# A searched instruction list, PSUM readers in turn, and filler matmuls behind a branch, in a four-layer graph kernel

## The chip, the cores and the metric

The kernel runs on one core of one Trainium2 chip. The metric is the device time of one execution in microseconds (us); lower is better. The kernel before takes 1670.46 us, the median of three runs (1670.09 to 1670.70).

## The reference

Thirty-two graphs of 512 nodes with 128 features each pass through four residual layers. All layers use the same 512x512 matrix `adj` of zeros and ones.

```python
# layer 0: edge scores
h   = relu(layernorm(x));  xh = elu(h @ Wi + bi)
e   = sigmoid(xh @ We_tgt[:, None] + xh @ We_src[None, :] + be) * mask(adj)
own = xh * e.sum(-1)
recv = elu(concat(e @ xh, own) @ Wn + bn)
x  += concat(recv, xh) @ Wm + bm
# layer 1: five steps of a gated update, h = relu(layernorm(x)) at the start
m = adj @ h;  z, r = sigmoid(gates of m, h);  c = tanh(m-part + (r*h) @ u5.T)
h = (1 - z) * h + z * c          # five times, then x += h
# layer 2: x += adj @ (relu(layernorm(x)) @ W) + b
# layer 3: x += sum over k of adj^k @ h @ W_k, k = 0..3
```

## The kernel before

**Staging.** The kernel never loops on the chip. Python code lists some thousand operations, each on a whole 128x512 tile or a piece of it, and a planner written in the kernel (class `Plan`) turns the list into one order, which is then emitted as it stands. Each operation (`Op`, made by `Plan.op`, L61) has an engine, a guessed duration, a due time, the values it reads and writes, and with these the operations that must be listed before it. `Plan.order` (L121) is a list scheduler: it walks through planned time, and whenever an engine is free it gives that engine the ready operation with the earliest due time, provided that buffers are free. The due times come from a pace: one graph begins every 14 us at first (`FIRST_PACE`) and every 56 us later (`PACE`). Many graphs are therefore under way at the same time, each in another layer.

The order of each engine's queue is fixed when the program is built. On the chip, semaphores alone decide when an instruction starts; an instruction that waits holds up everything behind it on its own engine. The planner's guessed times never appear on the chip.

**Buffers.** PSUM has eight banks, the kind `b`. One of them, `spare`, is taken out of the pool at L304 and serves as the target of filler matmuls: `plan.idle` (L306, printed as line L307) multiplies `ones` by `ones`. In the part of the list before the branch the planner puts a filler wherever TensorE has nothing to do. The bank goes back into the pool at planned time `BRANCH` = 18 us (L738).

**The branch.** The kernel counts whether `adj` survives rounding to a shorter format (L520, L541, L546; the count is `inexact`). The operations planned for the first 18 us stand ahead of a branch on that count (L1003, L1004). Behind it stand two arms, one for an exact and one for an inexact matrix. With the data at hand the exact arm runs. All later work is in the arm.

**Layer 0 of the first graphs** is what the early part consists of. For each graph: a product with `Wi` (L449), the first `elu`, a product with the token weights (L593), a spread of the scores (L630), four tanh (L645) and four masked products on VectorE (L648), four matmuls that gather messages (L656), a product with `ones` or `ones_r` for the sums (L449, L690), the value `own` (L693), a product with `Wn` (L449), the second `elu`, whose last step (L566) is the value `recv`, and eight matmuls with `Wm` (L703) whose sum is added to x (L469). The transposed weights of layer 1 are made on the way (L761, L763), and a permuted copy of the matrix, AQ (L845, L848).

**elu** (L549 to L568) reads one PSUM bank three times: exp and tanh on ScalarE, and the linear part, max(v + bias, 0). The linear part is VectorE's (L559) for the first two graphs' first elu and ScalarE's (L562) everywhere else.

**Steady work.** Layer 1's step has five products with a 128x128 weight (L449: u3T, w4T, w3T, w5T, u5T), eight fp32r matmuls with the matrix (L857), copies out of PSUM by ScalarE (L438), sums by VectorE (L882 and others). Layer 3 is L938 and L947.

Of the kernel before, what the change touches and what calls it, by code (L numbers as in the profile page):

```python
# [2 lines left out]

# [38 lines left out]
class Plan:  # L42
# [7 lines left out]
    def __init__(self, slots, ahead, last):  # L50
        self.ahead, self.last, self.ops, self.vals = ahead, last, [], {}
        self.free = {k: [(0.0, i) for i in range(n)] for k, n in slots.items()}
        self.until = dict.fromkeys(self.RESULT, 0.0)
        self.shared, self.now = 0.0, 0.0
        self.careful = 0.0
        self.slack = 0.0
        self.pieces = {}
        self.cold = 4.5
        self.idle = None

    def op(self, eng, us, due, emit, reads=(), writes=(), two=None, keep=0, result=None,  # L61
           earliest=0.0, margin=0.0):

        two = eng == "POOL" if two is None else two
        o = Op(eng, us, self.RESULT[eng] if result is None else result, emit, two, keep)
        o.earliest, o.margin = earliest, margin
        for v in reads:  # L70
            o.before.add(v.writer)
        for v in writes:
            o.before.update(v.readers)
            if v.writer:
                o.before.add(v.writer)
            elif v.kind and v.slot is None:
                o.takes.append(v)
        for v in reads:
            v.readers.append(o)
        for v in writes:  # L80
            v.writer, v.readers = o, []
        o.vals = [v.whole or v for v in dict.fromkeys([*reads, *writes])]
        for v in o.vals:
            v.left += 1
        for v in [*reads, *writes, *o.vals]:
            self.vals[v] = True
        o.before -= {o, None}
        o.due = max([due, *(b.due for b in o.before)])
        for b in o.before:
            b.after.append(o)  # L90
        self.ops.append(o)
# [28 lines left out]
    def order(self, end=None):  # L120

        left = [o for o in self.ops if not o.begun]
# [5 lines left out]
        coming, ready = {e: [] for e in self.until}, {e: [] for e in self.until}  # L128
        order, events, index = [], [self.now], {}
# [25 lines left out]
        while events:  # L155
            now = heapq.heappop(events)
            if end is not None and now >= end:
                break
            for e in self.until:
                while coming[e] and coming[e][0][0] <= now:  # L160
                    _, i, o = heapq.heappop(coming[e])
                    heapq.heappush(ready[e], (o.due, i, o))
                if self.until[e] > now:
                    continue
                passed, o = [], None
                while ready[e] and o is None:
                    x = heapq.heappop(ready[e])
                    if begins(x[2], now):
                        o = x[2]
                    else:  # L170
                        passed.append(x)
                for x in passed:
                    heapq.heappush(ready[e], x)
                if o is not None and now < self.careful and any(
                    c.due < o.due and t < now + 0.3 * o.us for t, _, c in coming[e]
                ):
                    heapq.heappush(ready[e], (o.due, index[o], o))
                    o = None
                if o is None and e == "PE" and end is not None and self.idle.known <= now:
                    order.append(self.idle)  # L180
                    self.until[e] = now + self.idle.us * (1.9 if now < self.cold else 1.0)
                    heapq.heappush(events, self.until[e])
                if o is None:
                    continue
                order.append(o)
                o.begun = True
                while oldest + 1 < len(by_due) and by_due[oldest].begun:
                    oldest += 1
                o.start, self.until[e] = now, now + o.us
                if o.two:  # L190
                    self.shared = self.until[e]
                for v in o.takes:
                    v.slot = self.free[v.kind].pop(self.clean(now) if v.added else 0)[1]
                    if v.kind == "b":
                        self.pieces[v.slot] = v.pieces
                o.known = self.until[e] + o.result
                heapq.heappush(events, self.until[e])
                heapq.heappush(events, o.known)
                for v in o.vals:
                    v.left -= 1  # L200
                    if not v.left and v.kind:
                        self.free[v.kind].append((o.known, v.slot))
                        self.free[v.kind].sort()
                for a in o.after:
                    if a in index:
                        a.waits -= 1
                        a.ready = max(a.ready, self.known(o, a))
                        if not a.waits:
                            heapq.heappush(coming[a.eng], (a.ready, index[a], a))
                            heapq.heappush(events, a.ready)  # L210
        assert end is not None or len(order) == len(left), "the plan does not end: too few buffers"
        self.now = end or 0.0
        return order


@with_exitstack
def tile_four_graph_layers(
# [33 lines left out]
    assert D == P and G * D == 512 and N == 512 and K == 7  # L251

    PACE, FIRST_PACE, LAST_PACE = 56.0, 14.0, 30.0
    BRANCH = 18.0
    MARGIN = 10.0
    FIRST = 2

# [4 lines left out]
    plan = Plan(slots, ahead=60.0, last=(B - 2) * PACE)  # L262
# [33 lines left out]
    def chunks(t):  # L296
# [9 lines left out]
    plan.free["b"].pop()  # L306
    plan.idle = Op("PE", 0.224, 0.0, lambda: nc.tensor.matmul(  # L307
        spare[:, :P], at(ones), at(ones), start=True, stop=True), False, 0)
    plan.idle.known = 0.4
    op("POOL", 0.2, -9, lambda: nc.gpsimd.memset(at(neg_half), -0.5), [], [neg_half])  # L310
    ones_r = const("ones_r", [P, P], F32R)
    op("POOL", 0.4, 5, lambda: nc.gpsimd.tensor_copy(at(ones_r), at(ones)), [ones], [ones_r])
# [45 lines left out]
    Wm_sb = load_const(Wm.rearrange("(t p) o -> p t o", p=P), [P, 2, P], "Wm_sb", -5)  # L358
    bm_bc = load_const(bm.partition_broadcast(P), [P, P], "bm_bc", -5, earliest=BRANCH)
    load_graph(3, -6, 3.6)  # L360
# [362 lines left out]
    def issue(operations):  # L723
        with tc.manual_schedule():
            for o in operations:
                o.emit()
# [6 lines left out]
    def arm(exact):  # L733
        with ExitStack() as stack:
            pool = stack.enter_context(tc.tile_pool(name=f"arm{exact:d}", bufs=1))
            plan.back_to(common)
            plan.slack = 0.3
            plan.free["b"].append((BRANCH, len(places["b"]) - 1))  # L738
            list_rest(exact, pool)
            issue(plan.order())  # L740

    def list_rest(exact, pool):
        n = 25 if exact else 16
# [260 lines left out]
    with tc.If(taken < 1) as branch:  # L1004
        arm(True)
# [42 lines left out]
```

## Time and profile before

| | |
|---|---|
| three runs | 1670.09, 1670.46, 1670.70 us |
| profiled execution, its own time | 1668.0 us |
| its span, first to last instruction | 1666.2 us |
| outside the span | 1.8 us |
| TensorE clock granted | 1.0 throughout |
| end of the last matmul to the end of the span | some 5.3 us |

The profile is of one execution. PE is TensorE, DVE is VectorE, ACT is ScalarE, POOL is GpSimd and SP issues most of the DMAs. A row of a timeline gives start, length, engine, line, operation, tiles and a count; brackets give the engine's idle time just before it and what ended that. One fp32 product of 128x512 appears as two matmul records. A matmul's recorded length runs past the start of the next one, so the time that a matmul takes from the engine is read from one start to the next.

### The profile page before, as it was taken

The page shows a single profiled execution, that of the slowest core. Times are in us where ns is not written, and L with a number is a line of the kernel's source. Part 1 is how long each engine was busy: PE and PEld are TensorE (multiplying, and loading weights), DVE is VectorE, ACT ScalarE, POOL GpSimd, SP SyncE. Part 2 cuts the span into 40 slices and gives each one's busy share as a digit, 9 for nine tenths or more (in the row PEclk, how much of TensorE's full clock was granted, in tenths as well). Part 3 has the DMA queues.
Part 4 walks back from the last instruction along what each step waited for, and adds up shares of the span by engine and source line. Part 5 has one row for each costly group of instructions (what it writes and reads, how often), then busy time and mean ns, then how long its engine had stood idle before and what let it go on. Part 6 is the DMA issues. An engine that isn't in the chain of part 4 may idle for free.

```text
span 1666.2 us, 21483 instructions
## 1 busy us (share of the span) xinstructions
PE 1655.3 (99%) x6585; PEld 1071.5 (64%) x6585; DVE 1429.3 (86%) x3344; ACT 1131.0 (68%) x2133; POOL 237.7 (14%) x240
## 2 busy tenths in 40 slices
PE   9999999999999999999999999999999999999998
PEld 6555556656666666666666666666666666666787
DVE  8889999999988898889888898888999888877842
ACT  7877677877766677667666677676768666655640
POOL 2211101212111110111111111101121110000100
PEclk9999999999999999999999999999999999999999
DMA  3444434543445434454434454444454543222202
GB/s 99 122 112 142 133 113 109 134 123 112 133 115 139 123 112 114 105 137 127 127 102 112 123 134 115 120 117 118 129 137 128 127 126 96 89 64 89 83 14 60
DMA packets 284925, 188.05 MB, mean 113 GB/s; under 512 B 77312, under 2 KB 237952, under 8 KB 284800
## 3 DMA queue, kind: packets, MB, share of 16 engines
q1 hardware_dynamic: 270688, 162.98, 32.7%
q0 software_dynamic: 12528, 22.81, 8.2%
q8 instruction: 54, 0.88, 0.2%
q10 hardware_dynamic: 1584, 0.79, 0.2%
q14 instruction: 71, 0.58, 0.1%
HBM read 82.78 MB, written 73.33 MB: 94 GB/s over the span
## 4 chain that ended last, share of the span: by engine, by line
PE 97%; ACT 2%; DVE 1%; issue 0%; ACTq 0%; DVEq 0%
PE b L449 44%; PE b L857 21%; PE b L947 11%; PE b L938 7%; PE b L656 6%; PE b L703 3%; PE b L920 2%; PE b L593 2%; PE b L690 1%; PE b L307 1%; ACT f L495 0%; ACT f L454 0%; ACT f L645 0%; PE b L378 0%; DVE f L648 0%
## 5 line engine op out<-in xcount | busy, mean ns | idle before, releaser
L438 ACT COPY f<-b 128x512 f32<-128x512 f32 x356 | 206.5, 586 | 147.9 <-PE b L857 103.8
L857 PE MATMUL b<-AQ,r 128*128 128x512 f32 x1024 | 304.7, 439 | 0.0
L486 POOL TENSOR_TENSOR s<-s,nhalf 128x4 f32<-128x4 f32 x128 | 155.9, 1218 | 897.1 <-DVE s L484 795.9
L857 PEld LDWEIGHTS b<-AQ,r 128*128 128x128 f32 x1024 | 192.1, 188 | 90.2 <-issue 51.4
L882 DVE TENSOR_TENSOR f<-f,b 128x512 f32<-128x512 f32 x320 | 211.6, 676 | 26.7 <-PE b L449 24.8
L390 DVE STREAM_TRANSPOSE f<-f 128x512 f32<-128x512 f32 x246 | 206.7, 844 | 20.9 <-ACT f L495 20.3
L947 PE MATMUL b<-r,A_r 128*128 128x512 f32 x768 | 223.9, 426 | 0.0
L454 ACT ACTIVATE f<-f,b4w 128x512 f32<-128x512 f32 x160 | 115.3, 723 | 156.1 <-DVE f L882 155.4
L495 ACT ACTIVATE f<-x,s 128x128 f32<-128x128 f32 x504 | 207.3, 489 | 16.3 <-DVE s L490 16.0
L947 PEld LDWEIGHTS b<-r,A_r 128*128 128x128 f32 x768 | 139.3, 189 | 46.6 <-issue 24.4
L449 PE MATMUL b<-f,u3T 128*128 128x512 f32 x320 | 163.1, 593 | 1.1 <-DVE f L882 0.9
L449 PE MATMUL b<-f,w4T 128*128 128x512 f32 x320 | 163.1, 593 | 0.2 <-ACT f L438 0.2
L449 PE MATMUL b<-f,u5T 128*128 128x512 f32 x320 | 162.7, 592 | 0.2 <-DVE f L889 0.2
L449 PE MATMUL b<-f,w5T 128*128 128x512 f32 x320 | 162.4, 592 | 0.0
L449 PE MATMUL b<-f,w3T 128*128 128x512 f32 x320 | 162.2, 592 | 0.0
L857 PE MATMUL b<-A_r,r 128*128 128x512 f32 x512 | 149.0, 433 | 0.0
L899 DVE TENSOR_TENSOR f<-f,f 128x512 f32<-128x512 f32 x160 | 109.0, 681 | 43.2 <-ACT f L454 42.9
L938 PEld LDWEIGHTS b<-V,f 128*128 128x128 f32 x1024 | 131.0, 191 | 21.2 <-issue 15.6
L680 POOL DMA_DIRECT2D f<-f x87 | 78.0, 897 | 458.7 <-DVE r L831 71.7
L454 ACT ACTIVATE f<-b,b5w 128x512 f32<-128x512 f32 x160 | 109.5, 685 | 48.0 <-PE b L449 47.1
L831 DVE TENSOR_TENSOR r<-f,r 128x512 fp32r<-128x512 f32 x192 | 130.2, 680 | 8.3 <-ACT r L827 8.2
L454 ACT ACTIVATE f<-f,b3w 128x512 f32<-128x512 f32 x160 | 114.9, 720 | 27.2 <-DVE f L882 26.4
(112 smaller groups left out, 2539.8 us busy)
## 6 DMA issues: line engine op xcount, KB each, us to landing
m<-f SPq DMA_DIRECT2D x246, 256.0 KB, 2.1
f<-m SPq DMA_DIRECT2D x186, 256.0 KB, 2.9
f<-f POOLq DMA_DIRECT2D x87, 256.0 KB, 3.6
f<-m SPq DMA_DIRECT2D x240, 64.0 KB, 2.5
x<-in_x_dram SPq DMA_DIRECT2D x32, 256.0 KB, 3.3
f<-f SPq DMA_DIRECT2D x29, 256.0 KB, 2.4
f<-d SPq DMA_DIRECT2D x28, 256.0 KB, 5.3
out_dram<-x SPq DMA_DIRECT2D x28, 256.0 KB, 2.4
```

What stands on the lines that cost most here:

```text
L390: op("DVE", us, due, lambda: nc.vector.transpose(view_out(at(blocks)), view_in(at(src))), [src], [blocks])
L438: op("ACT", us, due, lambda: nc.scalar.copy(at(t), at(src)), [src], [t])
L449: nc.tensor.matmul(to, at(w), of, start=start, stop=stop)
L454: op("ACT", us, due, lambda: nc.scalar.activation(at(dst), at(src), AF.Tanh, bias=at(bias), scale=scale), [src, bias], [dst])
L486: op("POOL", 1.35, due, lambda: nc.gpsimd.tensor_tensor(stat(SCALE), stat(VAR), at(neg_half), op=ALU.pow), [s, neg_half], [s])
L495: nc.scalar.activation(at(h)[:, ts(c, P)], at(X[b])[:, c, :], AF.Relu, bias=stat(SHIFT)[:, c : c + 1], scale=stat(SCALE)[:, c : c + 1],)
L831: op("DVE", T_VEC, due, lambda: nc.vector.tensor_tensor(part(lo), whole(), part(hi).bitcast(F32), op=ALU.subtract), [src, hi], [lo], two=two)
L857: nc.tensor.matmul(at(pa), at(part)[:, ts(jc, P)], view(at(columns)[:, jc, :]), start=jc == n == 0, stop=jc == NC - 1 and n == PARTS - 1,)
L882: op("DVE", T_VEC, d, lambda: nc.vector.tensor_tensor(at(s), at(u), at(pg), op=ALU.add), [u, pg], [s])
L899: op("DVE", T_VEC, d, lambda c=c, h=h: nc.vector.tensor_tensor(at(c), at(c), at(h), op=ALU.subtract), [c, h], [c], two=True)
L938: nc.tensor.matmul(at(pz)[:, ts(i, D)], at(hT[i])[:, ts(ic, P)], at(V[k]), start=i == 0, stop=last and i == G - 1,)
L947: nc.tensor.matmul(at(pz), at(adjT)[:, jc, ts(ic, P)], at(part), start=False, stop=jc == NC - 1 and n == PARTS - 1,)
```

## The change

1. **Readers of a bank in turn.** `Plan.op` now also makes an operation that reads a PSUM bank come after the bank's previous reader, if that one is on another engine. For the first two graphs' first elu this puts the VectorE linear part behind exp and tanh.
2. **Filling behind the branch.** Fillers are planned up to time `FILL` = 50 us instead of up to the branch, and are left out if a TensorE operation becomes ready within one filler's length. The spare bank goes back into the pool at 50 us instead of 18 us.
3. **A searched list.** In the exact arm, the due times of all operations due before 130 us are varied at random 240 times (a shift for one engine or all in a stretch of time, or a shift for 1 to 10% of the operations). The planner lists the arm for each variant, and the variant whose planned end is earliest is kept. The search runs while the program is built and costs no device time.

The lines of `elu` itself are the same in both kernels: the linear part on VectorE for the first two graphs was there before.

```diff
     def op(self, eng, us, due, emit, reads=(), writes=(), two=None, keep=0, result=None,
...
         for v in reads:
             o.before.add(v.writer)
+            if v.kind == "b" and v.readers and v.readers[-1].eng != eng:
+                o.before.add(v.readers[-1])
...
-                if o is None and e == "PE" and end is not None and self.idle.known <= now:
+                if o is None and e == "PE" and self.idle.known <= now < self.fill and not (
+                    coming[e] and coming[e][0][0] < now + self.idle.us):
                     order.append(self.idle)
...
+    def searched_order(self, until, rounds):
+        ops = [o for o in self.ops if not o.begun]
+        early, rng, asked = [o for o in ops if o.due < until], random.Random(3), self.state()
+
+        def listed(due):
+            self.back_to(asked)
+            for o, d in zip(early, due):
+                o.due = d
+            return self.order()
+
+        best, first = None, [o.due for o in early]
+        due = first
+        for _ in range(rounds):
+            try:
+                listed(due)
+                end = max(o.start + o.us for o in ops)
+                if best is None or end <= best[0]:
+                    best = end, due
+            except AssertionError:
+                pass
+            due = [*best[1]]
+            if rng.random() < 0.5:
+                start, width = rng.uniform(15, until), rng.uniform(2, 15)
+                shift, eng = rng.gauss(0, 4), rng.choice(["PE", "ACT", "DVE", None, None])
+                varied = {i: shift for i, o in enumerate(early)
+                          if start <= first[i] < start + width and eng in (None, o.eng)}
+            else:
+                n = max(1, int(len(early) * rng.uniform(0.01, 0.1)))
+                varied = {i: rng.gauss(0, 4) for i in rng.sample(range(len(early)), n)}
+            for i, shift in varied.items():
+                due[i] += shift
+        return listed(best[1])
...
-    BRANCH = 18.0
+    BRANCH, FILL = 18.0, 50.0
...
-    plan.idle.known = 0.4
+    plan.idle.known, plan.fill = 0.4, FILL
...
-            plan.free["b"].append((BRANCH, len(places["b"]) - 1))
+            plan.free["b"].append((FILL, len(places["b"]) - 1))
             list_rest(exact, pool)
-            issue(plan.order())
+            issue(plan.searched_order(130.0, 240) if exact else plan.order())
```

The two built programs can be laid side by side, engine by engine. In the arm that runs, TensorE has the same 4469 matmul instructions in both, counted without fillers. Fillers: 46 before, all ahead of the branch; 69 after, 42 ahead of it and 27 behind. Their runs after the change are 21, 3, 3, 5, 2 and 8 ahead of the branch and 3, 1, 8, 9, 1 and 5 behind. The last 745 matmul instructions stand in the same order, kind by kind, in both.

More of the change, by code (lines that the diff above doesn't have):

```diff
@@ L2 @@
 import heapq
+import random
 import concourse.bass as bass
@@ L58, in __init__ @@
         self.cold = 4.5
+        self.fill = 0.0
         self.idle = None
@@ L210, in order @@
                             heapq.heappush(events, a.ready)
-        assert end is not None or len(order) == len(left), "the plan does not end: too few buffers"
+        assert end is not None or all(o.begun for o in left), "the plan does not end: too few buffers"
         self.now = end or 0.0
         return order
+    def searched_order(self, until, rounds):
[28 more added lines that the diff above has]
+        return listed(best[1])
 @with_exitstack
```

## The prediction

> **What bounds the kernel now.** First the page's engine shares and the chain of work that ended last:
>
> ```profile
> PE 1655.3 (99%) x6585; PEld 1071.5 (64%) x6585; DVE 1429.3 (86%) x3344; ACT 1131.0 (68%) x2133; POOL 237.7 (14%) x240
> ...
> PE 97%; ACT 2%; DVE 1%; issue 0%; ACTq 0%; DVEq 0%
> ```
>
> TensorE bounds the kernel. So the time is the matmuls' own time, which the change leaves alone, plus fillers, plus TensorE's stalls, plus the ends. Next TensorE's waits, all that the profile shows (total, times, longest):
>
> ```profile
> PE b L703 <- DVE f L566: 1.8, 2, 1.2
> PE b L307 <- DVE ones L302: 1.0, 1, 1.0
> PE b L449 <- DVE f L882: 0.9, 1, 0.9
> PE b L761 <- ACT f L562: 0.8, 1, 0.8
> PE b L656 <- DVE f L648: 0.3, 1, 0.3
> PE b L449 <- DVE f L889: 0.2, 1, 0.2
> PE b L449 <- ACT f L869: 0.2, 1, 0.2
> PE b L449 <- ACT f L438: 0.2, 1, 0.2
> ```
>
> Only 5.4 us in 1666. Asked by stretch, the waits for L566, L562, L648 and L869 (3.1 us) lie between 20 and 70 us, those for L882, L889 and L438 (1.3 us) between 350 and 400. Nothing else waits until the last matmul. A matmul's record outlasts its slot, so these numbers are too small; starts tell more. The timeline around the worst wait:
>
> ```profile
> 27.24 1.06 PE L593 MATMUL b<-W_tok,f 128*128 128x130 f32 x8
> 28.13 0.49 PE L761 MATMUL b<-ident,f 128*128 128x128 f32 x3
> 29.38 0.33 PE L761 MATMUL b<-ident,f 128*128 128x128 f32 x1 [0.76 <-ACT f L562]
> 29.64 0.65 PE L630 MATMUL b<-ident,s 128*128 128x128 f32 x4
> 31.51 2.05 PE L703 MATMUL b<-Wm_sb,f 128*128 128x128 f32 x16 [1.22 <-DVE f L566]
> 33.40 0.60 PE L378 MATMUL b<-ident,f 128*128 128x128 f32 x4
> ```
>
> Four L630 records take 0.44 us from start to start, so L703 could have begun at 30.1: the stall is 1.4 us, not 1.22. Taking the regular spacing of each kind (0.43 us per half product, 0.11 per 128-wide record, 0.23 per fp32r matmul) from all starts, the stalls are: 0.4 at L449 Wn (26.3), 1.1 around L761 (29.4), 1.5 at L703 (31.5), 0.3 and 0.1 at 36.5 to 41, 0.8 at the second L703 (46.0), 0.6 at L656 (62.1), 0.4 at u3T (63.5), with small remainders **5.4 us** between 20 and 70 us. From 350 to 400 us they are **2.1 us**, the largest here:
>
> ```profile
> 383.26 1.02 PE L449 MATMUL b<-f,Wi_sb 128*128 128x512 f32 x2
> 385.22 1.13 PE L449 MATMUL b<-f,u3T 128*128 128x512 f32 x2 [0.94 <-DVE f L882]
> ```
>
> That 7.5 us is all that a better order can remove; elsewhere TensorE is full. Fillers, of which all 46 lie before 18.9 us:
>
> ```profile
> 12.02 1.28 PE L307 MATMUL b<-ones 128*128 128x128 f32 x10
> 13.23 0.34 PE L541 MATMUL b<-ones,n_odd 128*1 128x1 f32 x8
> ```
>
> Five fillers take 1.21 us here; from filler to filler it is 0.22.
>
> **What the Trainium skill says.** "TensorE: Matmul & The Clock Gate", Part 1: the array starts at half clock, reaches full clock after about 3.4 us of work, and falls back only after an idle window of about 3.4 us. The trace agrees: filler records start 0.21 us apart until 5.7 us and 0.11 after. Behind the branch the longest idle is 1.22 us and the spacing after it stays at 0.11. So filling behind the branch has no clock to save.
> "PSUM — Partial Sum Buffer", PSUM bank collisions: two engines must not touch one bank at once, and software has to keep them apart, reads against reads too. The kernel's program did so already, without the planner's knowledge: ScalarE's exp waits for VectorE's linear part.
>
> ```profile
> 10.91 0.75 DVE L559 TENSOR_SCALAR f<-b,bi_sb 128x512 f32<-128x512 f32 x1 [1.60 <-PE b L449]
> ...
> 11.69 0.69 ACT L554 ACTIVATE f<-b,bi_sb 128x512 f32<-128x512 f32 x1 [0.57 <-DVE f L559]
> ```
>
> "Trainium Kernel Development and Optimization", Reading a trace, calls matmul busy time a bad metric because matmuls are pipelined. The trace agrees (L449's u3T records last 0.59 us on average at 0.43 spacing); hence starts above.
>
> **The change, part by part.**
> *Fillers.* 23 more, each an instruction that TensorE executes whether or not it would have waited: 23 x 0.222 = **+5.1 us**. Work that a stall would have covered hides them; without a stall they are pure cost.
> *Readers in turn* adds no wait on the chip that was not there. In graph 0's elu the linear part moves behind tanh. Before, L559, exp, tanh, L564 and L566 ran from 10.91 to 14.41. After, exp starts when ScalarE is through its last cast and mask scaling at about 10.8, tanh ends at 12.0, and VectorE, which has graph 1's normalization ahead (1.03 us of L501), does linear part, L564 and L566 from 12.5 to 14.3. The same end: 0.
> *The branch.* `inexact` now stands behind three mask steps and two score steps on VectorE: written at 14.4 before, about 16.6 after. SP issued its first load behind the branch 1.06 us after that (15.53), so all of SP's queue there (weights, biases, graphs 4 and 5) comes about 2.1 us later. The first users are VectorE's L759 and L481 and TensorE's L761 at 23.9 to 25.7; w4's load would land at about 19.2 + 2.9 = 22.1. Covered by 1.8 us. POOL, ACT, DVE and PE have work queued across the branch as before: 0.
> *The order.* I followed the new queues by the durations of this profile (VectorE 0.60 per full tile, ScalarE 0.57, statistics 1.26, a product 0.86, four transposes 0.44). Reaching the first L703, TensorE has done the same real work in both orders: before 31.51 - 8.30 - 24 fillers (5.3) - stalls 2.8 = 15.1 us. After, with one filler fewer at the start, it is 8.1 + 15.1 + 42 fillers (9.3) + 0.15 (a transpose waiting for graph 1's normalization) = **32.6**. Is `recv` there? Wn ends at 27.6, exp, tanh and linear part end at 29.5, L564 at 29.6, then the list has graph 3's statistics (1.26) ahead of L566: 31.5. The fillers outlast it by 1.1 us. Second L703: before 46.02, of it 13.0 real work since the first; after 32.6 + 13.0 + 6 fillers (1.3) = **46.9**; `recv` by ScalarE's queue (L495 for graph 1's layer 1 stands ahead of exp) at 46.0. Outlasted again, by 0.9. So stalls up to there vanish (4.3 us) and fillers take their place and more. Then up to 70 us I find the producers ahead of every use by 0 to 1 us, 0.2 us of stalls where 1.0 was. Sum at 70 us: +5.1 - 5.4 + 0.4 = **+0.1**. My walk can err by a microsecond per chain, and errors only add stalls: +0.4 taken, bounds -0.3 (no stall left) and +5.1 (all stalls stay).
> *Later.* Between 350 and 400 us the new list puts Wi earlier and other work between Wn and the next u3T, so the wait at 385 loses its place. But VectorE is 94% busy from 200 to 400 (140.5 us of 150, 47.2 of 50), and a list off by a little finds another wait. The trace does not show the new ones; bounds 0 and 4 us, taken 1.1 in place of 2.1: **-1.0**.
> *The ends.* The last 745 matmul instructions, 212 us by the spacings above, stand in the same order; the start's wait for `ones` stays: 0.
> Sum: +0.4 - 1.0 = **-0.6 us**. Against the profiled execution: span 1665.6, with the 1.8 us outside 1667.4. The profiled execution lies 2.5 us under the median of the runs, so I take the difference to the median: 1670.46 - 0.6 = **1669.9**.
>
> **The rivals.**
> *A. Fillers for stalls, later waits halved:* 1669.9, own range 1668.9 to 1671.1.
> *B. The later wait goes and none comes:* stalls at 70 us even, -2.1, with the walk's +0.1: 1668.4. For it: one place held nearly all of it, and the list changed there. Against: VectorE's load.
> *C. The later waits grow instead:* two or three waits of 1.2 us among VectorE's backlog between 60 and 480 us, +0.4 + 1.5: 1672.4.
> *D. Slower: fillers come on top of the stalls.* Place: the two L703. If `recv` is later than I found, by other waits on ScalarE's and VectorE's queues, TensorE runs its 27 fillers and still waits. With all stalls kept: 1670.5 + 5.1 = 1675.6. It decides from `recv` being late by the margins (1.1 and 0.9) plus about 3 us in sum. For it: a search fits the list to guessed times and leaves no slack. Against: the guesses (0.61, 0.6, 0.86) are near the measured durations.
> That the change does nothing to elu's linear part is plain from the diff; that item is no part of any sum.
>
> **How the numbers follow.** Measurement tells about 0.2% (3.3 us) from no change. A 0.50, B 0.22, C 0.18, D 0.10. Faster by over 0.2% needs 1667.1, below B's bound of -0.3 - 2.1 = 1668.1: 0.03 for what I overlook. Slower needs 1673.8: D and the far end of C less D's near end, 0.11. Range 1667.9 to 1673.4: it takes in A, B and most of C and leaves D out.
>
> **What would show it.** Right: L307 records 138 (twice 69), about 18 us in all; TensorE's waits for L566 and L562 gone or under 0.3 us; the first L703 at about 32.6, the second at 46.9; waits behind 70 us at most 2 us. Wrong: L703 still waiting behind its fillers (D), new waits of TensorE for VectorE between 60 and 480 us (C), or matmul spacings that changed.

## The result and the profile after

The changed kernel takes 1667.67 us, the median of 20 runs (1666.05 to 1668.86). The kernel before, run beside it, takes 1670.05 us (20 runs, 1667.43 to 1672.00). The ratio is 0.9987, 95% interval 0.9981 to 0.9993: faster by 2.4 us between the medians, and by 2.2 us (1.2 to 3.2) by the ratio, which is estimated from all the runs. The prediction said 1669.9 and a range from 1667.9, so the change gained about 2 us more than its sum, and the median lies 0.2 us under the range.

The profiled execution of after has an own time of 1666.99 us and a span of 1665.2. First the page's engine shares and the head of its chain of work:

```profile
PE 1657.5 (100%) x6631; PEld 1076.8 (65%) x6631; DVE 1428.9 (86%) x3344; ACT 1127.5 (68%) x2133; POOL 236.8 (14%) x240
...
PE 96%; DVE 2%; DMA 1%; ACT 1%; issue 0%; DVEq 0%
```

TensorE counts as busy for the whole span, rounded; the 46 more matmul records are the 23 fillers, each listed twice. The waits of TensorE in after, all that the profile shows (total, times, longest):

```profile
PE b L348 <- DVE ones L343: 1.0, 1, 1.0
PE b L697 <- DVE f L689: 0.5, 1, 0.5
PE b L634 <- DVE f L923: 0.2, 1, 0.2
```

Of the eight rows of before, the one for `ones` stays, the one for the masked product (L656 before, L697 now) stays, and the other six are gone. The one new row is 0.2 us at 384.6 us. The lines named here stand 41 lower down in the file than before. The timeline at the place where before had its worst wait (L802 is the transpose that was L761, L744 the product with `Wm` that was L703, L348 a filler):

```profile
28.12 0.27 PE L802 MATMUL b<-ident,f 128*128 128x128 f32 x1
28.23 1.95 PE L348 MATMUL b<-ones 128*128 128x128 f32 x16
30.02 0.27 PE L802 MATMUL b<-ident,f 128*128 128x128 f32 x1
30.13 2.17 PE L348 MATMUL b<-ones 128*128 128x128 f32 x18
32.14 0.27 PE L802 MATMUL b<-ident,f 128*128 128x128 f32 x1
```

Seventeen fillers (34 records) stand where TensorE waited before. `recv` for the first L744 is done at 31.50 (L607, 30.82 + 0.68), as predicted; L744 starts at 32.25, where 32.6 was predicted, without a wait. The second L744 starts at 46.60 (predicted 46.9).

The place of the worst later wait of before, at 385 us, looks like this in after (L490 was L449, L731 was L690, L634 was L593):

```profile
377.09 1.02 PE L490 MATMUL b<-f,Wi_sb 128*128 128x512 f32 x2
378.04 0.73 PE L731 MATMUL b<-q,ones_r 128*128 128x512 f32 x2
...
382.93 1.02 PE L490 MATMUL b<-f,u3T 128*128 128x512 f32 x2
383.79 0.61 PE L634 MATMUL b<-W_tok,f 128*128 128x130 f32 x4
384.64 0.71 PE L634 MATMUL b<-W_tok,f 128*128 128x130 f32 x4 [0.24 <-DVE f L923]
385.19 1.02 PE L490 MATMUL b<-f,w3T 128*128 128x512 f32 x2
```

The product with `Wi` now stands 6 us ahead of the one with `u3T`, which no longer waits. Instead the eight records of L634 take 1.40 us from start to start in place of 0.89: by starts, the new wait is 0.5 us and not 0.2.

So the early part went as predicted and brought nothing. To see where the gain is, I take the same accounting as the prediction's: TensorE's starts, less the regular spacing of each kind of matmul. What is left is waiting, cold start and a drift of my spacings of about 0.37 us per 100 us, the same in all kernels. The table gives it for three profiled executions of before and two of after (the repeats are experiments below); "tail" runs from the last matmul's start to the end of the span.

| us | fillers | waits to 70 us | 70 to 600 | behind 600 | last matmul starts | tail | span |
|---|---|---|---|---|---|---|---|
| before | 10.26 | 8.32 | 4.56 | 3.72 | 1660.47 | 5.73 | 1666.20 |
| before, second | 10.26 | 8.28 | 4.78 | 4.42 | 1661.35 | 6.52 | 1667.88 |
| before, third | 10.26 | 8.74 | 4.81 | 4.97 | 1662.39 | 6.49 | 1668.88 |
| after | 15.39 | 3.41 | 2.77 | 3.65 | 1658.84 | 6.35 | 1665.19 |
| after, second | 15.39 | 3.56 | 2.16 | 3.65 | 1658.37 | 5.94 | 1664.31 |

Fillers and early waits together: 18.6, 18.5, 19.0 before and 18.8, 18.95 after, a change of about +0.2 us by the means. These columns hold the cold start too: 22, 22 and 26 of the first filler records are about 0.21 us apart in place of 0.11 in before, 17 and 21 in after. By the means that is some 0.4 us in favour of after which the change did not make. Between 70 and 600 us: -2.25 by the means. Behind 600 us: -0.7. The gain is late. It lies in waits behind 70 us, while the last filler is planned for 50 us.

### The profile page after: what moved, and what is told of

Read it like the earlier page. It is cut to its first block, busy times and chain, and to the rows that moved or that the text cites. A ratio compares the mean times of both kernels' runs of the same rounds, so it can differ in the third digit from the quotient of the medians.

```text
span 1665.2 us, 21541 instructions
## 1 busy us (share of the span) xinstructions
PE 1657.5 (100%) x6631; PEld 1076.8 (65%) x6631; DVE 1428.9 (86%) x3344; ACT 1127.5 (68%) x2133; POOL 236.8 (14%) x240
## 4 chain that ended last, share of the span: by engine, by line
PE 96%; DVE 2%; DMA 1%; ACT 1%; issue 0%; DVEq 0%
PE b L490 43%; PE b L898 21%; PE b L988 11%; PE b L979 7%; PE b L697 6%; PE b L744 3%; PE b L961 2%; PE b L634 2%; PE b L348 1%; PE b L731 1%; DMA m<-f 0%; DVE f L431 0%; DVE f L923 0%; DVE r L872 0%; DMA f<-m 0%
## 5 line engine op out<-in xcount | busy, mean ns | idle before, releaser
L898 PEld LDWEIGHTS b<-AQ,r 128*128 128x128 f32 x1024 | 192.1, 188 | 89.4 <-issue 51.4
L490 PE MATMUL b<-f,w4T 128*128 128x512 f32 x320 | 163.2, 592 | 0.0
L490 PE MATMUL b<-f,u3T 128*128 128x512 f32 x320 | 163.1, 592 | 0.0
L490 PE MATMUL b<-f,u5T 128*128 128x512 f32 x320 | 162.9, 592 | 0.0
L490 PE MATMUL b<-f,w5T 128*128 128x512 f32 x320 | 162.8, 592 | 0.0
L490 PE MATMUL b<-f,w3T 128*128 128x512 f32 x320 | 162.3, 592 | 0.0
```

Source lines behind the costliest of these rows:

```text
L490: nc.tensor.matmul(to, at(w), of, start=start, stop=stop)
L898: nc.tensor.matmul(at(pa), at(part)[:, ts(jc, P)], view(at(columns)[:, jc, :]), start=jc == n == 0, stop=jc == NC - 1 and n == PARTS - 1,)
```

## The experiments

Medians beside the kernel before on the same chip; ratios with 95% intervals. The gain or loss in microseconds is the difference of the two medians; the ratio is estimated from all the runs, and differs from the quotient of the medians by up to 0.0005. Waits by stretch come from one profiled execution of each kernel.

**What comes and goes in the kernel before.** No edit.

> The kernel before, unchanged, profiled a second time. Theory T (TensorE is full, so the time is fixed matmul work plus fillers plus stalls, and the first profile, 2.5 us under the median, caught an execution with few stalls): median 1670.0, and the second profile shows another sum of stalls than the first, with the later stalls (60 to 600 us, 3.2 us in the first) differing by 1 us or more while the early ones (20 to 60 us) repeat within 0.3. Rival: stalls repeat within 0.3 us everywhere, and executions differ in what lies outside the matmuls.

1668.85 us against 1669.20, ratio 1.0003 (0.9995 to 1.0011). The waits up to 70 us repeat within 0.15 us and those at 358, 360 and 385 us within 0.05 us, so these belong to the list; the expected difference of 1 us or more before 600 us did not show. But the profile has two more, at 726 and 728 us, which its first profile lacks (the timeline of this execution):

```profile
726.09 1.12 PE L449 MATMUL b<-f,u5T 128*128 128x512 f32 x2
727.05 1.05 PE L938 MATMUL b<-V,f 128*128 128x128 f32 x8
728.31 1.12 PE L449 MATMUL b<-f,w4T 128*128 128x512 f32 x2 [0.20 <-ACT f L438]
```

By starts they and the ones beside them cost 0.77 us, and the tail is 0.8 us longer. So what differs between these two executions lies behind 600 us.

**Are the fillers behind the branch pure cost?** The fillers are taken out of, or doubled in, the finished list of the changed kernel, so that nothing else moves.

```diff
-            issue(plan.searched_order(130.0, 240) if exact else plan.order())
+            listed = plan.searched_order(130.0, 240) if exact else plan.order()
+            issue([o for o in listed if o is not plan.idle])
```

> The changed kernel with its 27 fillers behind the branch not emitted; order otherwise the same. Theory T: the fillers stand where TensorE would wait, and outlast the waits by 0.7 us (recv of graph 0 at 31.5, its matmuls at 32.25) and 0.6 us (46.0 and 46.6): without them waits of 4.7 us come back and the kernel gains 1.3 us, 1666.4. Rival F (filling itself brings the gain, by clock or otherwise): 1670 or slower. Rival P (fillers are pure cost): 6.0 us faster, 1661.7.

1667.85 us against 1669.20, ratio 0.9996 (0.9988 to 1.0005). It is not faster than the full change (0.9987) but, if anything, about 1 us slower, although 6.0 us of fillers are gone. The theory that they are pure cost falls. Theory T missed as well, by 1.4 us: it had no term for the clock. The timeline of this kernel shows the waits that came instead (L803 is the transpose, L744 the product with `Wm`):

```profile
29.21 0.33 PE L803 MATMUL b<-ident,f 128*128 128x128 f32 x1 [1.19 <-ACT f L603]
31.52 0.33 PE L803 MATMUL b<-ident,f 128*128 128x128 f32 x1 [1.98 <-ACT f L686]
31.68 3.25 PE L744 MATMUL b<-Wm_sb,f 128*128 128x128 f32 x16
34.73 0.98 PE L419 MATMUL b<-ident,f 128*128 128x128 f32 x4
```

Two waits of 3.2 us in sum, as expected of a list without fillers. But the sixteen L744 records take 3.05 us from 31.68 to 34.73, where before's sixteen take 1.89 (31.51 to 33.40). The stretches say why (columns: stretch, its length, TensorE's busy time and instructions, granted clock, DMA share, GB/s):

```profile
31.00:32.00 1.00, 0.48 (x4) 1.00 0.00 0
32.00:33.00 1.00, 1.00 (x7) 0.54 0.00 0
33.00:34.00 1.00, 1.00 (x7) 0.50 0.00 0
34.00:35.00 1.00, 1.00 (x7) 0.50 0.00 0
35.00:36.00 1.00, 1.00 (x6) 0.75 0.00 0
```

TensorE ran at half clock from 32 to 35.5 us: 0.46 + 0.50 + 0.50 + 0.25 = 1.7 us lost, behind waits of which none was over 2 us by the records. Up to 70 us the waits of this kernel are 10.51 us against 3.41 with the fillers: 7.1 us more, of it 1.7 from the clock, for 6.0 us of fillers saved.

```diff
-            issue(plan.searched_order(130.0, 240) if exact else plan.order())
+            listed = plan.searched_order(130.0, 240) if exact else plan.order()
+            issue([x for o in listed for x in ([o, o] if o is plan.idle else [o])])
```

> The changed kernel with each of the 27 fillers behind the branch emitted twice. Theory T: no wait is left for them to stand in, so they cost their length, 27 x 0.222 = 6.0 us: 1673.7. Rival (fillers are hidden by something): under 1670.

1672.28 us against 1669.20, ratio 1.0020 (1.0012 to 1.0029). 27 x 0.222 = 6.0 us of fillers are added, the waits up to 70 us stay (3.51 against 3.41), and the last matmul starts 5.5 us later than in after, the rest being 0.6 us less between 70 and 600. Where nothing waits any more, a filler is paid in full.

**One part of the change at a time.** From the kernel after, each part is undone by one of these edits; for the readers in turn alone, that part was added to the kernel before.

No readers in turn:

```diff
-            if v.kind == "b" and v.readers and v.readers[-1].eng != eng:
-                o.before.add(v.readers[-1])
```

No filling behind the branch:

```diff
-                if o is None and e == "PE" and self.idle.known <= now < self.fill and not (
-                    coming[e] and coming[e][0][0] < now + self.idle.us):
+                if o is None and e == "PE" and end is not None and self.idle.known <= now:
...
-    BRANCH, FILL = 18.0, 50.0
+    BRANCH, FILL = 18.0, 18.0
```

No search:

```diff
-            issue(plan.searched_order(130.0, 240) if exact else plan.order())
+            issue(plan.order())
```

Search alone (readers in turn and filling undone):

> The kernel before with the searched list alone: no readers in turn, fillers (46) only ahead of the branch, spare bank back at 18 us. Theory T: the search shortens some of the 5.4 us of early stalls and moves the later ones; 1668.5, between the two kernels. Rival S (the searched list is the whole gain, the other two parts cost): 1667.0 or below. Rival N (without readers in turn the search fits a plan that does not hold): 1670 or slower, with early stalls of 5 us or more.

Filling and readers in turn, no search:

> The changed kernel without the search: readers in turn and fillers behind the branch (35 in the arm, 42 ahead of it, 77 in all), list as the planner first makes it. Theory T2 (the gain is waits behind 70 us that the searched list does not have; up to 70 us fillers and stalls trade evenly): no gain, 1669.0 to 1671.0 on the scale where the kernel before takes 1669.2 to 1670, with waits of 1.5 us or more between 70 and 600 us. Rival (turns and fillers bring the gain): 1667.7 or below.

Readers in turn alone:

> The kernel before with readers in turn alone, no search, fillers (43) only ahead of the branch. Theory T2: within 1 us of the kernel before, unless the list behind 70 us happens to change, in which case by the change of the waits there. Rival C (readers in turn makes a worse list): 1.5 us slower or more.

Readers in turn and search, no filling:

> Readers in turn and search, fillers (43) only ahead of the branch, bank back at 18 us. Theory T2: as the search alone, 3 to 4 us faster than the kernel before (ratio 0.998), waits behind 70 us under 0.7 us. Rival C (readers in turn costs what the full change lacks against the search alone): ratio 0.9987 like the full change. If it is as fast as the search alone, it is the fillers and the withheld bank that cost the full change its 1.4 us.

Filling alone:

> Fillers behind the branch and the bank withheld until 50 us, alone: no readers in turn, no search (42 fillers ahead of the branch, 23 behind). Theory T3 (fillers cost their length, 19 more than in the kernel before = 4.2 us, and take the place of waits; they gain only where the waits would drop the TensorE clock, which the list of the kernel before does not do): fillers and waits up to 70 us sum to 18.6 to 19.6 us as against 18.6, time within 1.5 us of the kernel before. Rival F (filling gains by itself): 2 us faster.

Filling and search, no readers in turn:

> The full change without readers in turn. Theory T3: the gain is the search's, and without readers in turn the list is as good as with the search alone: 3 to 4 us faster than the kernel before, full clock throughout. Rival C2 (readers in turn is what makes the search's plan hold once fillers are there): no faster than the full change, ratio 0.9987 or above.

| parts | median, before beside it | ratio (interval) | fillers + waits to 70 us | 70 to 600 | behind 600 |
|---|---|---|---|---|---|
| search alone | 1665.42, 1669.20 | 0.9978 (0.9972 to 0.9985) | 17.97 | 2.14 | 3.93 |
| filling + search | 1666.36, 1668.82 | 0.9982 (0.9975 to 0.9990) | 19.70 | 2.08 | 3.65 |
| all three (the change) | 1667.67, 1670.05 | 0.9987 (0.9981 to 0.9993) | 18.80 | 2.77 | 3.65 |
| filling alone | 1670.06, 1668.82 | 1.0004 (0.9995 to 1.0012) | 18.90 | 5.45 | 3.65 |
| filling + turns | 1670.77, 1669.13 | 1.0007 (0.9999 to 1.0016) | 20.85 | 2.83 | 5.44 |
| turns alone | 1671.15, 1669.13 | 1.0013 (1.0005 to 1.0021) | 23.58 | 4.17 | 3.66 |
| turns + search | 1671.84, 1669.13 | 1.0016 (1.0008 to 1.0023) | 20.94 | 7.00 | 4.01 |

The "fillers + waits" column holds the cold start: from 14 (filling alone) to 29 (turns + search) of the first filler records at half-clock spacing, by an estimate from these counts up to 1.5 us between two rows, so smaller differences in that column tell nothing.

The gain is the search's: every kernel that is faster than before has it, and taking it from the change takes the gain away (filling + turns, 1.0007). The search alone is the fastest of all by its median, 3.8 us under before; its interval and the change's just overlap. A search is no warrant of a gain, though: with the readers in turn and no filling it is slower than before, against both expectations. Of the others, rival S held for the search alone and rival C for turns alone, and filling + search gained 2.5 us where 3 to 4 were expected.

Filling alone gives nothing that can be told from none. Readers in turn alone cost 2.0 us. They bunch the waits: in its profile, an execution 1.75 us over its median, between 30 and 50 us that kernel waits 1.10, 1.68, 1.58 and 0.67 us, and the clock falls to half twice (34.3 to 37.8 and 48 to 51.4 us). The stretches of that execution:

```profile
34.00:35.00 1.00, 1.00 (x8) 0.67 0.00 0
35.00:36.00 1.00, 1.00 (x7) 0.50 0.00 0
36.00:37.00 1.00, 1.00 (x4) 0.50 0.00 0
37.00:38.00 1.00, 1.00 (x3) 0.62 0.00 0
48.00:49.00 1.00, 1.00 (x5) 0.50 0.59 174
49.00:50.00 1.00, 1.00 (x7) 0.50 0.06 16
50.00:51.00 1.00, 1.00 (x6) 0.50 0.00 0
51.00:52.00 1.00, 1.00 (x8) 0.80 0.00 0
```

With the search but without fillers, the readers-in-turn kernel has one wait of 2.86 us at 33.6, one stretch at half clock after it (34.6 to 38.0 us), and some 4.4 us of new waits between 70 and 130 us; this profile lies 1.6 us over its median. With fillers the readers' order has no cost that can be told (all three against filling and search: the intervals overlap). So the parts do not add. What the filling does for the readers' order is shown in part: added to turns + search it takes 2.1 us off up to 70 us (some 1.2 of it the cold start), where it keeps the clock, but 4.2 us off between 70 and 600 us, where there are no fillers and the search found another list. Whether that is the filling's doing or the luck of another list was not tried.

The table shows one thing more. Against filling + turns, the list without the search, the change gains 2.05 us up to 70 us (some 0.5 of it the cold start) and 1.8 us behind 600, and little between (2.83 against 2.77). That the search gains in the later waits holds against the kernel before.

**Does any search do it, or this one?** The seed of the random variation is 4 in place of 3.

```diff
-        early, rng, asked = [o for o in ops if o.due < until], random.Random(3), self.state()
+        early, rng, asked = [o for o in ops if o.due < until], random.Random(4), self.state()
```

Search alone with seed 4:

> The search alone with another random sequence (4 in place of 3). Theory T2 with a search that works: 2.5 to 4 us faster than the kernel before, waits behind 70 us under 0.7 us again. Rival L (luck: any other list has other waits): anywhere from 1 us slower to 4 us faster, waits behind 70 us of 1 us or more.

1667.25 us against 1669.13, ratio 0.9988 (0.9982 to 0.9995). Half the gain of seed 3: this list keeps a wait of 1.0 us for L927 behind 70 us, and its waits from 70 to 600 us are 3.79 against 2.14. Half of the gain hangs on the random sequence; theory T2 (2.5 us or more) missed, and the time lies in rival L's range.

The full change with seed 4:

> The full change with another random sequence in the search (4 in place of 3). Theory T3: up to 70 us as the full change within 1.5 us, since the fillers hold the clock; behind 70 us other waits, between 0 and 3 us more: ratio 0.998 to 1.001. Rival (the change gains whatever the sequence): ratio 0.9987 within 0.0006.

1667.63 us against 1668.82, ratio 0.9993 (0.9985 to 1.0001). Its waits from 70 to 600 us are the lowest of all (1.85), but 16.28 us of fillers were planned. The search alone has the sign of seed 3 at half the size; the full change with seed 4 cannot be told from no change, as its interval takes in 1.

A variation without choosing: the due times of 5% of the early operations are varied once, and that list is taken.

```diff
...
+        due = [o.due for o in early]
+        for i in rng.sample(range(len(early)), len(early) // 20):
+            due[i] += rng.gauss(0, 4)
+        return listed(due)
```

> The kernel before with one random variation of its due times (a twentieth of the operations due before 130 us, shifts of 4 us standard deviation), taken without looking at the planned end: a list changed without a search. Theory T3 (the search does choose: lists not chosen are worse): waits up to 130 us longer than in the kernel before by 2 us or more, 1671.5 or slower. Rival L (any other list would do, the later waits of the kernel before were bad luck): 1666 to 1669.

1669.76 us against 1668.82, ratio 1.0005 (0.9997 to 1.0014). One blind variation does not help; its waits from 70 to 600 us are 6.18. The time missed both expectations. A single sample does not show that choosing by the earliest planned end is what helps, but it speaks for it. The profiles say more on what a list gains and loses. The waits between 350 and 400 us, by starts, are 2.2 us in before, and fall in most other lists, searched or not: 0.8 in this blind one, 0.4 with turns alone, 0.0 with filling + turns. But those three have 3.7, 2.0 and 1.05 us of waits between 70 and 350 us, where before has 0.2, while the change has 0.2, filling + search 0.4 and the search alone 0.45. Losing the wait at 385 us is easy; gaining few others is what these faster lists have besides. This kernel shows a second thing. It has the two waits around 30 us of before, to the hundredth (its L781 and L723 are before's L761 and L703):

```profile
29.86 0.33 PE L781 MATMUL b<-ident,f 128*128 128x128 f32 x1 [0.76 <-ACT f L582]
30.13 0.65 PE L650 MATMUL b<-ident,s 128*128 128x128 f32 x4
32.00 3.43 PE L723 MATMUL b<-Wm_sb,f 128*128 128x128 f32 x16 [1.22 <-DVE f L586]
```

But L723's records take 3.22 us to the next start, where before's sixteen took 1.89, and the stretches of the same execution say why:

```profile
32.00:33.00 1.00, 1.00 (x6) 0.71 0.00 0
33.00:34.00 1.00, 1.00 (x7) 0.50 0.00 0
34.00:35.00 1.00, 1.00 (x6) 0.50 0.00 0
35.00:36.00 1.00, 1.00 (x8) 0.59 0.00 0
```

So waits of 0.76 and 1.22 us with 0.55 us of matmuls by their spacing between them can halve the clock, and need not: three profiles of before, one of the search alone and one of the late search below keep 1.00 over the same two waits (0.8 and 1.2 us).

**Early list or late list?** The search alone once more, allowed to vary only the operations due from 50 to 130 us, or only those due before 50 us.

```diff
-        early, rng, asked = [o for o in ops if o.due < until], random.Random(3), self.state()
+        early, rng, asked = [o for o in ops if 50.0 <= o.due < until], random.Random(3), self.state()
```

> The kernel before with the search alone (no readers in turn, no fillers behind the branch), and the search may vary only operations due between 50 and 130 us. Theory W: the gain of the search lies in TensorE's waits behind 70 us (some 3.8 of 8.3 us by starts), not in the early part. Then this kernel keeps the waits of before up to 50 us (0.76 and 1.22 us at 29 to 31.5) and is 2 to 3 us faster than before, ratio 0.9980 to 0.9988. Theory V: the gain of the search comes from the early list or from an accident of the whole list; then this kernel lies within 1 us of before, ratio 0.9994 to 1.0006, and the waits at 358 to 386 stay.

1666.27 us against 1668.93, ratio 0.9983 (0.9976 to 0.9990). All the waits of TensorE that its profile shows:

```profile
PE b L741 <- DVE f L604: 1.8, 2, 1.2
PE b L345 <- DVE ones L340: 1.0, 1, 1.0
PE b L799 <- ACT f L600: 0.8, 1, 0.8
PE b L694 <- DVE f L686: 0.2, 1, 0.2
```

The early waits of before are all there (1.8 and 0.8 us at the product with `Wm` and the transpose), no wait behind 70 us is listed, and the gain is 2.7 us: by the median as large as the whole change's.

```diff
-            issue(plan.searched_order(130.0, 240) if exact else plan.order())
+            issue(plan.searched_order(50.0, 240) if exact else plan.order())
```

> The kernel before with the search alone, and the search may vary only operations due before 50 us. Theory W: the early part has little to give, since the early waits hardly fell under the search over all operations (0.6 us by starts), so within 1 us of before, ratio 0.9994 or more, unless the shifted early list also moves what comes behind 70 us, which the waits at 358 to 386 would show by going. Theory V: 2 to 4 us faster, ratio 0.9976 to 0.9988, with the gain ahead of 70 us.

1669.53 us against 1668.93, ratio 1.0004 (0.9996 to 1.0013). No gain, and the wait of before at 385 us is still there, in the same order of work (the timeline of this kernel; L920 was L882):

```profile
385.00 1.12 PE L487 MATMUL b<-f,u3T 128*128 128x512 f32 x2 [0.94 <-DVE f L920]
```

For the search alone the two together show where the gain comes from: the order of what is due behind 50 us, not the early list. Each is one random sequence.

**How much do two executions of one kernel differ?** No edits: before a third time, after a second time, one execution each.

> The kernel before unchanged, one more execution with a profile. Theory W: executions of the same kernel differ by things that come and go at the same waits: a stretch of 3.4 us at half clock behind the waits at 29 to 31.5 us (1.7 us, mean clock 0.998), an extra wait at 726 us (0.8 us), a tail longer by up to 0.9 us. So its own time is between 1667.4 and 1671, and what it has over 1668.0 is found in these places. Rival: the waits at 29 to 31.5 never lower the clock in this kernel, and what differs is spread over the whole span.

Own time 1670.73 us. The clock stays at 1.00 from 8 to 70 us, so the half-clock stretch was not caught in this kernel. Instead the start is 0.45 us longer, with more of the first fillers at half clock, the wait at 358 us is missing, the one at 577.8 us is 0.7 us by starts, and a wait for a DMA stands at 1144.7, which neither other profile has (the timeline):

```profile
1142.78 0.83 PE L938 MATMUL b<-V,f 128*128 128x128 f32 x6
1144.71 0.46 PE L938 MATMUL b<-V,f 128*128 128x128 f32 x2 [1.09 <-DMA f<-m]
```

> The changed kernel unchanged, one more execution with a profile. Theory W: no stretch at half clock, since fillers stand where the waits were; the waits up to 70 us repeat within 0.2 us; own time between 1666 and 1668.9, and what it has over 1667.0 lies in the tail or in one wait behind 70 us. Rival: it too shows a stretch at half clock, and then the smaller spread of its times has another reason.

Own time 1666.10 us. No stretch at half clock; the wait at 62.8 us is 0.4 us where the first profile has 0.5, the 0.2 at 384.6 is no longer listed (0.25 us by starts, where the first has 0.5), and behind 600 us nothing differs (3.65 both times).

## Why the prediction was wrong, step by step

**Fillers, +5.1 us: right.** 69 fillers, 138 records; by starts 5.13 us more.

**The early waits, -5.4 + 0.4: right.** They fell by 4.9 us; with the fillers +0.2 on the first pair of profiles, where +0.1 was worked out and +0.4 taken (without the luck of the cold start some +0.6 by the means). Both L744 came 0.3 us ahead of the predicted times, both `recv` at the predicted ones. The 0.3 us are luck: the first matmul that is no filler starts at 7.61 us in this profile, where 8.1 was reckoned, because five fewer filler records than in before fell into the cold start. Rival D was wrong by this: the fillers outlasted `recv` by 0.75 us at the first L744 and 0.6 at the second.

**Readers in turn 0, the branch 0: right for the end.** SP issued its first load behind the branch at 17.48 us and nothing waited for it. But "no part of any sum" was too quick for the readers' order in general: without fillers it costs 2.0 us. With fillers no such cost can be told.

**The later waits, -1.0: the step that failed, by size.** The mechanism was right, the wait at 385 lost its place. The sum was too small in two places. I give the waits by starts here, against the spacing between the same kinds of neighbours, so that the drift drops out.

Between 350 and 400 us they are 2.2, 2.2 and 1.7 us in the three profiles of before and 0.9 and 0.3 in the two of after: -1.4 by the means, where "1.1 in place of 2.1" was taken. The first profile of after fits the 1.1, the second does not. I had reckoned with new waits because VectorE is 94% busy from 200 to 400 us. VectorE stayed as busy (191.7 us of these 200 against 187.8), and new waits did come (at 366, 378 and 384 us), but smaller ones.

The larger fault is "Nothing else waits until the last matmul". It was read from the list of waits; the starts show 0.5, 0.65 and 1.2 us between 400 and 600 us in before (at 436, 577 and 585 us) and none in after: another -0.8, which the prediction put at nothing. The two make the -2.25 us by the means of all profiles (-1.8 on the first pair).

This leans to rival B, which I gave 0.22, but B had its whole gain between 350 and 400 us and no new wait there. A busy producer was no sign of a late one: the list chosen by its planned end has fewer waits behind 70 us in most of its forms (from the tables, drift included: 1.9 to 2.8 us in five of the seven lists that a search over the later operations gave, 3.79 and 7.00 in the other two; 2.8 to 6.2 in the five lists without any search).

**Nothing behind 600 us: failed, and with it "so I take the difference to the median".** I priced the waits from one execution that lay 2.5 us under the median, and took what it lacked for something outside the change's reach. Two more profiles of before show what it lacked: 0.7 and 1.25 us of waits behind 600 us, and 0.8 us of tail. After shows none of those waits in two profiles, nor do the two kernels that have its list with no fillers or twice the fillers behind the branch. The means give -0.7 us. That the change removes these waits is not shown: the first profile of before has none either, and why they come in some executions only was not tried.

The terms again with the measured sizes: +0.2 - 2.25 - 0.7 = -2.75 us at the last matmul, and the tails differ by -0.1; measured medians differ by 2.4 us and the ratio's interval runs from 1.2 to 3.2. The predicted range began at 1667.9, just under B's lower bound; 0.7 us more behind 600 would have held the result.

**The base: 0.4 us too high.** 1670.46 was the median of three runs. Beside the changed kernel, 20 runs of the kernel before have a median of 1670.05. From there the same sum gives 1669.45 and a range from 1667.5, and the result lies in it: still 1.8 us from the forecast, so the sum above was too small, but that it fell outside the range is the base's share.

**"Filling behind the branch has no clock to save": failed as a rule, small in this change.** I took from the Trainium skill, "TensorE: Matmul & The Clock Gate", Part 1, that only an idle window of about 3.4 us brings the half clock back. The runs differ: idle of 1.19 and 1.98 us with a transpose between, or of 0.76 and 1.22 us with five 128-wide records between, was enough. The same page says two things that I passed over. Part 1 calls the window free-running, which fits that the same waits halve the clock in one execution and not in another. And its section "A second HAM failure mode: psum-queue depth-cycling" tells of short idle times between groups of matmuls that are frequent enough to do it; the experiments with bunched waits agree. What decides it stays open: of 21 executions of the search alone, whose profile has the same two waits as the blind variation, none reports a mean clock of 0.998 or less, of 13 of the blind variation six do. For the kernel before it weighs little. Of 179 executions that stood beside the experiments, 20 report a mean clock of 0.998 or less, and they are 1.6 us longer (1670.47 against 1668.90 us on average); one half-clock stretch is 1.7 / 1668 = 0.001 of the mean clock, and so fits. That is 0.2 us of the average. Of 91 executions of kernels with fillers behind the branch, none reports under 0.999; without fillers it is 7 of 13 with the readers' order alone and 8 of 13 in the changed list. That the 20 have this stretch is argued from these sums: no profile of before caught it.

## What to carry to other kernels

When TensorE is 99% full, ask of a reordering which waits far behind the edited stretch it moves, and test it by letting it touch only one part of the list: here, for the search alone, the early part gave nothing, and the part due behind 50 us gave 2.7 us, through waits as late as 385 us. Count waits by starts before calling a stretch free of them: the list of waits of the first profile showed none between 400 and 600 us, where the starts show 0.5. A profile that lies well under its kernel's median can lack some of the waits that other executions have, so profile the kernel again before pricing what a change can save. Filler matmuls were paid for in full where nothing waited, and earned their price only where the waits were bunched closely enough to halve the clock; searching the list without them and without the readers in turn had the lower median here with both random sequences (0.9978 and 0.9988, against 0.9987 and 0.9993), though the intervals overlap.

## What the runs showed of the hardware

In five stretches of four profiles the granted clock fell to 0.5, each time for about 3.4 us, by the stretches' figures, and so at a cost of 1.7 us. They came behind waits of 0.76 and 1.22 us, of 1.19 and 1.98 us, of 1.10 and 1.68 us, of 1.58 and 0.67 us (each pair within some 4 us), or of a single 2.86 us, and began within 1 us of the end of the last wait (32.4 to 35.8 us behind the first pair, 32.1 to 35.5 us behind the second). Behind waits of about 0.8 and 1.2 us the clock fell in one profile and not in five others. No profile with fillers in these places shows it.

The cold start varies: the first 22 fillers took 7.26 us from 1.04 to 8.30 in one profile of before and 7.71 us in another. Over all the profiles, 14 to 29 of the first filler records are about 0.21 us apart, and the rest 0.11. The recorded clock does not show it: in before it reads 1.00 from 0 to 10 us, so the "1.0 throughout" of the table of before says nothing of the start.
